# Two attention layers on one core: all casts to fp16 on GpSimd, the remainders' subtractions spread over later steps, and scores issued ahead of the row sums

## The chip, the cores and the metric

The program runs on 1 NeuronCore of a Trainium2 chip. The metric is the device time of one execution in microseconds; before and after are each run several times, and the median counts.

## The reference, cut to what matters

The input is 8 images of 512 channels by 32 x 32 positions (1024 tokens). Two attention layers follow each other. Layer 0 has 8 heads of 64 channels with quantized q, k and v; layer 1 has a single head over all 512 channels.

```python
# layer 0, per image: xf is (512, 1024)
h = group_norm(xf, gn_w, gn_b)
qkv = einsum('oc,bct->bot', qkv_w, h) + qkv_b
q, k, v = (fake_quant(t) for t in split(qkv))     # 8 bits, one scale over all images
w = softmax(einsum('bct,bcs->bts', q * scale, k * scale))
a = einsum('bts,bcs->bct', w, v)
x = xf + proj_w @ a + proj_b
# layer 1, per image
t = group_norm(x).reshape(B, C, H * W).transpose(0, 2, 1)
q, k, v = t @ wq.T + bq, t @ wk.T + bk, t @ wv.T + bv
out = softmax(q @ k.T / sqrt(C)) @ v
x = x + (out @ wp.T + bp)
```

## The kernel before, in words

The program has three parts. The first (up to about 640 us) normalizes all images, computes layer 0's q, k and v, stores them in device memory and gathers the extremes that the quantization needs; it is not touched by the change. The second and third are one interleaved stream: layer 0's attention, written as a Python generator `attention()`, and everything else (first the folding of layer 1's weights, `fold()`, then per image layer 0's output projection, `project`, the normalization `norm1`, and layer 1, `layer1`), written as generators too. Around 790 us the folding is over; until then the variable `alone` is true.

**Attention's units.** A unit is one image b, one pair of heads j, one half hf of the queries (512 of them) and one of 8 blocks s of 128 keys. There are 8 x 4 x 2 x 8 = 512 units. For each one:

- `scores` (L770 and above): two matmuls, one for each head of the pair, give `st`, 128 keys x 2 x 512 queries, in PSUM. ScalarE's exponential (L770) writes it to SBUF as `pt` in fp32. The pool of `st` tiles has two buffers, so the third unit's scores wait for the first one's exponential.
- the split: `pt` is cast to fp16 (L777), and VectorE subtracts the cast from `pt` (L778), again to fp16. The two fp16 parts together, tile `two`, stand for the fp32 value. The cast is on ScalarE for even s; for odd s it is on GpSimd, or on VectorE while `alone`.
- `weighted`: four matmuls per unit multiply both parts by v (`av`), and four sum them over the keys with a matrix of ones (`sm`), the softmax's denominators.
- `finish`, after the 8th block: ScalarE copies `av` and `sm` out of PSUM, and the division follows (L832), put off by some steps.

**Bursts.** The generator yields after every four units. One such step, a burst, issues the scores of two units, the `av` and `sm` matmuls of the four units of the burst before, and the scores of two more units. A burst that falls into the projection or the normalization is `dense` and is ordered in two halves of two units. In layer 1, the function `run` calls a burst where a block of products has reached a listed step.

**Layer 1's blocks.** Each matrix product of layer 1 is a 2 x 2 block scheme with seven products (`seven`), which accumulate in two PSUM banks x and y by turns. Between them ScalarE copies a bank to `kept_u` (L1055, L1092, L1188), and VectorE adds bank y and a kept copy into the result (L1068 for `g`, L1110 for `v`, L1125 for `p`, L1159 for the output). TensorE's next product but one into the same bank waits until that add has read it. In the list of products: the add for bank y of products 0 and 1 comes before product 3; the next before product 6; the last before the next block's product 1.

**Chores.** Work that can wait is put in a list by `later(name, delay, work)`, with the step at which it is due, and `chore()` takes the first entry that is due; `settle(name)` does all that is left under a name. While `alone`, `later` does the work at once. Quantization (L652, L655), division (L832) and some of the sums of layer 1 are chores. The splits of a burst's third and fourth unit are chores under the name "sum", due at once, cast and subtraction together; those of the first and second are issued right with their scores.

TensorE runs its instructions in the order in which the source issues them: `mm` (L106) ties each matmul to the last. On the other engines the framework's scheduler may order the queue otherwise than the source[...].

Of the kernel before, what the change touches and what calls it, by code (L numbers as in the profile page):

```python
# [9 lines left out]
F32 = mybir.dt.float32  # L10
BF = mybir.dt.bfloat16
F16 = mybir.dt.float16
I32 = mybir.dt.int32
AF = mybir.ActivationFunctionType
ALU = mybir.AluOpType
AX = mybir.AxisListType

P = 128
# [3 lines left out]
NT = T // P  # L22
# [31 lines left out]
def attn_pair_kernel(  # L54
# [9 lines left out]
    nc = tc.nc  # L64
# [5 lines left out]
    const = ctx.enter_context(tc.tile_pool(name="const", bufs=1))  # L70
# [26 lines left out]
            sq = slice(r, r + 32)  # L97
            nc.vector.tensor_tensor(gavg[sq, sq], low[sq, :], low_t[sq, :], ALU.is_equal)
    nc.vector.tensor_scalar(gavg, gavg, 1.0 / GS, None, ALU.mult)
    ident = const.tile([P, P], F32, name="ident")  # L100
    make_identity(nc, ident)

    last_mm = [None]

# [78 lines left out]
    with ExitStack() as fast:  # L183
# [84 lines left out]
        with tc.tile_pool(name="p1w", bufs=1) as p1w, tc.tile_pool(name="p1", bufs=3) as p1, tc.tile_pool(  # L268
            name="p1o", bufs=4
# [271 lines left out]
            for t in range(2 * PAIRS):  # L541
                isk, j = divmod(t, PAIRS)
# [96 lines left out]


        qkp = fast.enter_context(tc.tile_pool(name="qkp", bufs=2))
        ptp = fast.enter_context(tc.tile_pool(name="ptp", bufs=3))
        partp = fast.enter_context(tc.tile_pool(name="partp", bufs=6))
        aop = fast.enter_context(tc.tile_pool(name="aop", bufs=5))
        l2p = fast.enter_context(tc.tile_pool(name="l2p", bufs=1))
# [74 lines left out]
        chores = []  # L720
        now = 0

        def later(name, delay, work):
            if alone:
                work()
            else:
                chores.append((name, now + delay, work))

        def chore(passed=1):
            nonlocal now  # L730
            now += passed
            for i, (_, due, work) in enumerate(chores):
                if due <= now:
                    del chores[i]
                    work()
                    break

        def settle(what):

# [6 lines left out]
        def attention():  # L746

            units = [(b, j, hf, s) for b in range(B) for j in range(PAIRS) for hf in range(NH)
                     for s in range(NT)]
            pairs = {}
            pairs[0, 0] = load_pair(0, 0)
            parts, avs, sms, rss = {}, {}, {}, {}

            def scores(u, wait=False):
                b, j, hf, s = units[u]
                if hf == 0 and s == 0:
                    settle("quant")  # L760
                nm = f"{b}_{j}_{hf}"
                qt, kt, _ = pairs[b, j]
                st = pair_ps(f"st_{nm}_{s}")
                for i, r in enumerate(HALF):
                    mm(
                        st[:, i, :], lhsT=kt[r, bass.ts(s, P)],
                        rhs=qt[r, bass.ts(hf, 512)], start=True, stop=True,
                    )
                pt = ptp.tile([P, 2, 512], F32, tag="p", name=f"pt_{nm}_{s}")
                nc.scalar.activation(pt, st, AF.Exp, scale=esc)  # L770
                parts[u] = two = partp.tile([P, 2, 2, 512], F16, tag="two", name=f"two_{nm}_{s}")
                cast = nc.scalar.copy
                if s % 2:
                    cast = nc.vector.tensor_copy if alone else nc.gpsimd.tensor_copy

                def split():
                    cast(two[:, 0], pt)  # L777
                    nc.vector.tensor_tensor(two[:, 1], pt, two[:, 0], ALU.subtract)  # L778

                if wait:  # L780
                    later("sum", 0, split)
                else:
                    split()

            def weighted(us):
                for u in us:
                    b, j, hf, s = units[u]
                    if s == 0:
                        avs[b, j, hf] = av_bank(f"av_{b}_{j}_{hf}")
                    for w in range(2):  # L790
                        for i, r in enumerate(HALF):
                            mm(
                                avs[b, j, hf][r, :], lhsT=pairs[b, j][2][:, s, r],
                                rhs=parts[u][:, w, i, :], start=(s == 0 and w == 0),
                                stop=(s == NT - 1 and w == 1),
                            )
                for u in us:
                    b, j, hf, s = units[u]
                    if s == 0:
                        sms[b, j, hf] = av_bank(f"sm_{b}_{j}_{hf}")  # L800
                    two = parts.pop(u)
                    for n in range(4):
                        mm(
                            sms[b, j, hf][n * QUAD : (n + 1) * QUAD, :], lhsT=ones16,
                            rhs=two[:, n // 2, n % 2, :], start=(s == 0), stop=(s == NT - 1),
                        )

            def finish(b, j, hf):

                nm = f"{b}_{j}"  # L810
                if hf == 0:
                    ao[b, j] = aop.tile([P, NH, 512], F32, tag="ao", name=f"ao_{nm}")
                    rss[b, j] = l1p.tile([P, NH, 512], F32, tag="rs", name=f"rs_{nm}")
                aot, rs = ao[b, j], rss[b, j]
                nc.scalar.copy(aot[:, hf, :], avs.pop((b, j, hf)))
                nc.scalar.copy(rs[:, hf, :], sms.pop((b, j, hf)))
                if hf == 0:
                    return
                del rss[b, j]
                n = b * PAIRS + j  # L820

                apart = small.tile([P, 2, 16], F32, tag="apart", name=f"apart_{nm}")
                for w in range(2):
                    nc.sync.dma_start(
                        apart[:, w, :],
                        rs[2 * w * QUAD : 2 * (w + 1) * QUAD : QUAD].rearrange(
                            "r h (p k) -> r h p k", k=16
                        ),
                    )

                def divide():
                    nc.vector.scalar_tensor_tensor(aot, aot, scl[:, 2:3], rs, ALU.mult, ALU.mult)  # L832

                def spread():
                    r = rcs[:, n * 16 : (n + 1) * 16]
                    nc.vector.tensor_add(r, apart[:, 0, :], apart[:, 1, :])
                    nc.vector.reciprocal(r, r)
                    nc.sync.dma_start(rs_d[n].rearrange("r (p k) -> (r p) k", k=16), r)
                    for i, r in enumerate(HALF):
                        nc.sync.dma_start(  # L840
                            rs[r], rs_d[n][2 * i : 2 * i + 2, :].partition_broadcast(CH)
                        )
                    later("ao", 5, divide)

                later("ao", 4, spread)

            scores(0)
            scores(1)
            yield 9.0, 0
            scores(2)  # L850
            scores(3)
            yield 9.0, 0
            for u in range(0, len(units), 4):
                b, j, hf, s = units[u]
                settle("sum")
                if hf == 0 and s == 0:
                    n = b * PAIRS + j + 1
                    if n < B * PAIRS:
                        pairs[divmod(n, PAIRS)] = load_pair(*divmod(n, PAIRS))

                if u + 4 < len(units):
                    scores(u + 4)
                    scores(u + 5)
                weighted((u, u + 1) if dense else range(u, u + 4))
                late = dense
                for n in range(2):
                    if n == late:
                        if dense:  # L870
                            weighted((u + 2, u + 3))
                        if s == NT - 4:
                            finish(b, j, hf)
                    if n == 0 and u + 4 < len(units):
                        scores(u + 6, wait=True)
                        scores(u + 7, wait=True)
                chore(0)
                last = (j, hf, s) == (PAIRS - 1, NH - 1, NT - 4)
                yield 6.0 + (hf == NH - 1 and s == NT - 4), b + last
# [258 lines left out]
        def o_run(b, hf, vt, vs, ps_, pts, acc, rx, between):  # L1138
# [11 lines left out]
            nm = f"o2_{b}_{hf}"  # L1150
            spare = done >= B
            u = kept(nm, spare)
# [32 lines left out]
            for step in seven(  # L1185
# [20 lines left out]
                elif step == 6:  # L1206
# [6 lines left out]
                        check_sums()  # L1213
                    if (1, 0) not in rx:
                        load_x1(b, hf, 1, 0, rx)
                if step != 6:
                    chore(2)
            finish(1)
            settle("o")

# [11 lines left out]
        def run(*blocks, at=(5,)):  # L1232

            for steps in zip(*blocks):
                if steps[0] in at:
                    yield 1
                if len(blocks) > 1 and steps[0] == 6:
                    for _ in range(3):
                        chore(0)
                elif steps[0] not in (5, 6):  # L1240
                    chore()

        def layer1(b, steps):

# [182 lines left out]
        alone = True  # L1427
# [403 lines left out]
```

## Time and profile before

| | |
|---|---|
| time, median of 3 runs | 2819.06 us (2813.53 to 2820.5) |
| profiled execution | 2813.1 us span |
| TensorE busy | 2621.5 us, 93% |
| VectorE busy | 1924.6 us, 68% |
| ScalarE busy | 1152.1 us, 41% |
| GpSimd busy | 280.9 us, 10% |
| subtractions of the split (L778) | 512, mean 1236 ns, 617.1 us |
| exponentials (L770) | 512, mean 1124 ns, 554.7 us |
| casts on ScalarE, GpSimd, VectorE (L777) | 256, mean 1055 ns; 218, mean 1197 ns; 38, median 686 ns |

PE is TensorE, PEld its loading of weights, DVE is VectorE, ACT is ScalarE, POOL is GpSimd. A busy share is an average over stages with different limits; the ends of matmuls are modelled, and spans on GpSimd are rough. A span on VectorE or GpSimd can contain time in which the instruction was held up after it had begun. The page also names, for idle time, what ended it.

### The profile page before, as it was taken

Reading aid. Unit: us, or ns where it says so; the run is one execution under the profiler, and the core shown is the slowest. Engines: PE = TensorE matmul, PEld = TensorE weight load, DVE = VectorE, ACT = ScalarE, POOL = GpSimd, SP = SyncE. Lnnn points to the kernel's source line nnn. Section 1 sums busy time; section 2 is a strip of 40 time slices with the busy share of each in tenths; the row PEclk is TensorE's granted clock in tenths of the full one; section 3 lists DMA queues with packets and bytes.
Section 4 is the critical chain, followed back from the end, with each engine's and each line's share of the span. In section 5 each row is a group of like instructions: output and inputs, shape, how many; then the busy total and the mean of one; then the engine's idle time right before and its main releaser. Section 6 shows DMA issues by size and latency. Waiting matters only on the chain.

```text
span 2813.1 us, 33256 instructions
## 1 busy us (share of the span) xinstructions
PE 2621.5 (93%) x13110; PEld 1650.1 (59%) x13110; DVE 1924.6 (68%) x2772; ACT 1152.1 (41%) x1474; POOL 280.9 (10%) x248
## 2 busy tenths in 40 slices
PE   7999999997779999999999999999999999999998
PEld 3455555552226665665566566656665665567687
DVE  6766665668987767776776677677767766764534
ACT  0011111117955563645465455535563645463021
POOL 0000000000011111111111111111111111110000
PEclk9999999999999999999999999999999999999999
DMA  5233322333321223123212421241233123201401
GB/s 195 101 120 120 113 112 90 120 118 122 106 87 31 72 85 107 54 72 117 76 39 64 128 72 39 85 131 44 73 92 98 52 72 113 71 10 46 142 8 43
DMA packets 147461, 241.94 MB, mean 86 GB/s; under 512 B 26592, under 2 KB 92128, under 8 KB 145760
## 3 DMA queue, kind: packets, MB, share of 16 engines
q1 hardware_dynamic: 116448, 181.50, 19.5%
q10 hardware_dynamic: 30848, 58.23, 6.3%
q8 instruction: 104, 1.70, 0.3%
q14 instruction: 61, 0.50, 0.1%
HBM read 152.86 MB, written 86.28 MB: 85 GB/s over the span
## 4 chain that ended last, share of the span: by engine, by line
PE 50%; DVE 22%; issue 11%; ACT 10%; DMA 5%; POOL 1%; ACTq 0%; SPq 0%; DVEq 0%; POOLq 0%
PE s L106 10%; PE qkps L106 10%; DVE two L778 9%; PE o L106 7%; ACT pt L770 5%; PE pj L106 5%; PE vps L106 5%; PE v2ps L106 4%; PE g L106 4%; ACT two L777 3%; PE av L106 3%; DMA rs<-rs_d 2%; PE st L106 2%; PE sm L106 1%; DVE ao L832 1%
## 5 line engine op out<-in xcount | busy, mean ns | idle before, releaser
L778 DVE TENSOR_TENSOR two<-pt,two 128x1024 f16<-128x1024 f32 x512 | 617.1, 1236 | 254.8 <-ACT two L777 240.4
L770 ACT ACTIVATE pt<-st,esc 128x1024 f32<-128x1024 f32 x512 | 554.7, 1124 | 214.9 <-PE st L106 168.8
L777 POOL CAST two<-pt 128x1024 f16<-128x1024 f32 x218 | 260.9, 1197 | 1537.5 <-ACT pt L770 1531.7
L777 ACT CAST two<-pt 128x1024 f16<-128x1024 f32 x256 | 270.0, 1055 | 1.1
L106 PE MATMUL av<-two,v 128*64 128x512 f16 x2048 | 255.9, 388 | 0.3
L398 ACT ACTIVATE u<-qkps,qkb 128x512 f32<-128x512 f32 x84 | 57.7, 687 | 476.5 <-PE qkps L106 472.1
L106 PE MATMUL s<-g,h 128*128 128x256 f32 x1024 | 238.2, 382 | 13.7 <-DVE p L1125 10.1
L106 PE MATMUL pj<-ao,wp 128*128 128x512 f32 x512 | 223.0, 594 | 0.0
L106 PEld LDWEIGHTS s<-g,h 128*128 128x128 f32 x1024 | 191.7, 190 | 51.1 <-DVE p L1125 16.6
L106 PE MATMUL st<-q,k 64*128 64x512 bf16 x1024 | 166.1, 386 | 56.6 <-ACT pt L770 44.1
L106 PE MATMUL s<-g,sums 128*128 128x256 f32 x768 | 183.7, 386 | 14.3 <-ACT kept_u L1092 14.3
L106 PEld LDWEIGHTS <-v 128*64 128x64 f16 x2048 | 104.5, 110 | 134.4 <-issue 62.5
L106 PE MATMUL o<-p,v 128*128 128x256 f32 x768 | 174.1, 382 | 0.0
L106 PEld LDWEIGHTS s<-g,sums 128*128 128x128 f32 x768 | 142.0, 190 | 50.0 <-ACT kept_u L1092 22.7
L106 PE MATMUL qkps<-x,wqkv 128*128 128x512 f32 x352 | 165.4, 613 | 2.2 <-DVE x L155 2.2
L106 PEld LDWEIGHTS pj<-ao,wp 128*128 128x128 f32 x512 | 96.6, 190 | 119.0 <-issue 115.2
L106 PEld LDWEIGHTS o<-p,v 128*128 128x128 f32 x768 | 144.2, 190 | 27.2 <-issue 8.5
L106 PE MATMUL g<-h,wa 128*128 128x256 f32 x512 | 127.8, 394 | 30.7 <-DVE kept_u L1159 14.4
L106 PE MATMUL qkps<-sums,wa 128*128 128x512 f32 x336 | 153.3, 592 | 0.0
L106 PE MATMUL sm<-two,ones 128*32 128x512 f16 x2048 | 141.2, 387 | 0.0
L106 PEld LDWEIGHTS <-k 64*128 64x128 bf16 x1024 | 35.2, 94 | 174.3 <-issue 173.7
L106 PE MATMUL v2ps<-wm,h 128*128 128x256 f32 x512 | 121.9, 385 | 10.9 <-DVE v L1110 6.6
(218 smaller groups left out, 3530.6 us busy)
## 6 DMA issues: line engine op xcount, KB each, us to landing
rs<-rs_d SPq DMA_DIRECT2D x80, 256.0 KB
x<-in_x_dram SPq DMA_DIRECT2D x32, 512.0 KB
raw<-q_d SPq DMA_DIRECT2D x32, 512.0 KB
raw<-k_d SPq DMA_DIRECT2D x32, 512.0 KB
raw<-v_d SPq DMA_DIRECT2D x32, 512.0 KB
x_d<-h SPq DMA_DIRECT2D x64, 256.0 KB
x<-x_d ACTq DMA_DIRECT2D x64, 256.0 KB
out_dram<-x SPq DMA_DIRECT2D x64, 256.0 KB
```

Of the source, the lines that this page charges most:

```text
L106: ins = nc.tensor.matmul(*args, **kw).ins
L398: nc.scalar.activation(dst, x, AF.Identity, bias=bias)
L770: nc.scalar.activation(pt, st, AF.Exp, scale=esc)
L777: cast(two[:, 0], pt)
L778: nc.vector.tensor_tensor(two[:, 1], pt, two[:, 0], ALU.subtract)
L832: nc.vector.scalar_tensor_tensor(aot, aot, scl[:, 2:3], rs, ALU.mult, ALU.mult)
```

## The change

Five edits, made together.

- All casts of the split go to GpSimd; only while `alone` the odd ones are on ScalarE. None is on VectorE.
- `scores` no longer splits. A new function `split(u, delay)` issues the cast at once and puts the subtraction into the chores under "sum" with a delay: 0 for the burst's first two units, 1 for the other two.
- `chore` may now do several entries in a call: as many "sum" entries as steps have passed (at least one), and one entry of any other name unless it is called with `quiet`. Steps of a block that had no chore call now have a quiet one, so that a subtraction can stand there.
- `weighted` is divided into `over_keys` (the `av` matmuls) and `totals` (the `sm` matmuls). In a burst that isn't dense, the scores of the third and fourth unit are issued between the two, ahead of the row sums.
- The pool of `pt` tiles has four buffers instead of three, and an identity tile of the first part that nothing in this path read is gone.

It is meant to free ScalarE of the casts, to keep the subtractions from standing in front of layer 1's adds on VectorE, and to let the last two exponentials of a burst begin earlier.

```diff
-        ptp = fast.enter_context(tc.tile_pool(name="ptp", bufs=3))
+        ptp = fast.enter_context(tc.tile_pool(name="ptp", bufs=4))
...
-        def chore(passed=1):
+        def chore(passed=1, quiet=False):
             nonlocal now
             now += passed
-            for i, (_, due, work) in enumerate(chores):
-                if due <= now:
-                    del chores[i]
-                    work()
-                    break
+            for n in range(max(passed, 1) + (not quiet)):
+                for i, (name, due, work) in enumerate(chores):
+                    if due <= now and (name == "sum") == (n < max(passed, 1)):
+                        del chores[i]
+                        work()
+                        break
...
-                parts[u] = two = partp.tile([P, 2, 2, 512], F16, tag="two", name=f"two_{nm}_{s}")
-                cast = nc.scalar.copy
-                if s % 2:
-                    cast = nc.vector.tensor_copy if alone else nc.gpsimd.tensor_copy
-
-                def split():
-                    cast(two[:, 0], pt)
-                    nc.vector.tensor_tensor(two[:, 1], pt, two[:, 0], ALU.subtract)
-
-                if wait:
-                    later("sum", 0, split)
-                else:
-                    split()
+                pts[u] = pt
+
+            def split(u, delay):
+                b, j, hf, s = units[u]
+                pt = pts.pop(u)
+                two = partp.tile([P, 2, 2, 512], F16, tag="two", name=f"two_{b}_{j}_{hf}_{s}")
+                parts[u] = two
+                cast = nc.scalar.copy if alone and s % 2 else nc.gpsimd.tensor_copy
+                cast(two[:, 0], pt)
+                later("sum", delay, lambda: nc.vector.tensor_tensor(
+                    two[:, 1], pt, two[:, 0], ALU.subtract
+                ))
...
-                weighted((u, u + 1) if dense else range(u, u + 4))
-                late = dense
-                for n in range(2):
-                    if n == late:
-                        if dense:
-                            weighted((u + 2, u + 3))
-                        if s == NT - 4:
-                            finish(b, j, hf)
-                    if n == 0 and u + 4 < len(units):
-                        scores(u + 6, wait=True)
-                        scores(u + 7, wait=True)
+                two_scores(u + 4)
+                if dense:
+                    over_keys((u, u + 1))
+                    totals((u, u + 1))
+                    two_splits(u + 4, 0)
+                    two_scores(u + 6)
+                    over_keys((u + 2, u + 3))
+                    totals((u + 2, u + 3))
+                else:
+                    over_keys(range(u, u + 4))
+                    two_scores(u + 6)
+                    totals(range(u, u + 4))
+                    two_splits(u + 4, 0)
+                if s == NT - 4:
+                    finish(b, j, hf)
+                two_splits(u + 6, 1)
                 chore(0)
...
-                if step != 6:
-                    chore(2)
+                chore(2, quiet=step == 6)
...
-                elif steps[0] not in (5, 6):
-                    chore()
+                else:
+                    chore(quiet=steps[0] in (5, 6))
```

## The prediction

> **What bounds the kernel now.** I read the page's busy line first, then busy time by stretches of time, then TensorE's waits, then groups of instructions by form, then the timeline of single bursts. The columns are: engine shares on the page; in the stretches the length, then PE, PEld, DVE, ACT and POOL busy with counts, clock, DMA share and GB/s; in the waits total us, times, longest.
>
> ```profile
> PE 2621.5 (93%) x13110; PEld 1650.1 (59%) x13110; DVE 1924.6 (68%) x2772; ACT 1152.1 (41%) x1474; POOL 280.9 (10%) x248
> ...
> 640.00:790.00 150.00, 112.28 (x805) 37.32 (x802) 143.37 (x170) 128.92 (x139) 0.00 (x0) 0.94 0.31 103
> ...
> 1381.00:1642.00 261.00, 244.23 (x1382) 160.11 (x1379) 184.44 (x230) 133.76 (x170) 39.08 (x33) 0.99 0.26 79
> ```
>
> TensorE bounds the whole (93%), but there are two regimes. From 640 to 790 us attention runs almost alone: VectorE is busy 143.37 of 150 us, TensorE only 112.28, so VectorE is the limit there. From 800 us on, an image repeats every 261 us with TensorE at 244 and VectorE at 184. TensorE's own waits from 800 us to the end name VectorE or ScalarE as the releaser:
>
> ```profile
> PE sm_l L106 <- DVE acc L1293: 19.0, 7, 2.7
> PE g L106 <- DVE kept_u L1159: 14.4, 13, 2.0
> PE s L106 <- ACT kept_u L1092: 14.3, 21, 0.7
> PE s L106 <- DVE p L1125: 10.1, 13, 1.3
> ```
>
> So layer 1's products stop now and then for an add on VectorE (L1125, L1110, L1159, L1068: they empty a PSUM bank that the next product but one overwrites). Little of that is lost now, but the adds are just in time. One burst of the repeating image, with its columns start, length, engine, line, operation, tiles, shape, count, idle time before:
>
> ```profile
> 1448.42 0.60 PE L106 MATMUL st<-q,k 64*128 64x512 bf16 x4
> ...
> 1449.01 2.13 ACT L770 ACTIVATE pt<-st,esc 128x1024 f32<-128x1024 f32 x2
> ...
> 1451.01 1.05 ACT L777 CAST two<-pt 128x1024 f16<-128x1024 f32 x1
> 1451.19 1.38 POOL L777 CAST two<-pt 128x1024 f16<-128x1024 f32 x1 [9.90 <-ACT pt L770]
> ...
> 1452.10 2.68 DVE L778 TENSOR_TENSOR two<-pt,two 128x1024 f16<-128x1024 f32 x2 [0.43 <-ACT two L777]
> ...
> 1454.70 0.68 DVE L1125 TENSOR_TENSOR p<-s,kept_u 128x512 f32<-128x512 f32 x1
> ```
>
> Two exponentials, one cast on ScalarE beside one on GpSimd, two subtractions, then the add that TensorE needs, 6.96 us after the burst's first matmul; the third product needs it at 7.7. The other two casts and subtractions come behind that add.
>
> And how GpSimd and VectorE meet (q, k quantization and a cast; then division, cast, and an add out of PSUM):
>
> ```profile
> 1439.65 0.75 DVE L655 TENSOR_SCALAR q<-raw,bhi 128x1024 bf16<-128x1024 f32 x1
> 1439.87 1.43 POOL L777 CAST two<-pt 128x1024 f16<-128x1024 f32 x1 [2.36 <-ACT pt L770]
> 1440.31 1.53 DVE L655 TENSOR_SCALAR k<-raw,bhi 128x1024 bf16<-128x1024 f32 x1
> ...
> 1414.09 1.28 DVE L832 SCALAR_TENSOR_TENSOR ao<-ao,scl,rs 128x1024 f32<-128x1024 f32 x1
> ...
> 1414.31 1.96 POOL L777 CAST two<-pt 128x1024 f16<-128x1024 f32 x1 [2.36 <-ACT pt L770]
> 1415.29 0.68 DVE L1110 TENSOR_TENSOR v<-v2ps,kept_u 128x512 f32<-128x512 f32 x1
> ```
>
> The cast alone takes 1.04 us. Started during q (which ends at 1440.40) it ends at 1441.30, 0.90 after q; k, caught behind it, takes 1.53 instead of 0.75 and ends 0.54 after the cast. The cast behind the division ends 0.90 after it too (1415.37, 1416.27), while the add out of PSUM runs its normal 0.68 within that cast. So SBUF work of the two engines goes one at a time. In the burst above the first subtraction ends about 1.07 after the cast that held it (1452.57; the pair ends at 1454.78, the second takes 1.14).
>
> [...]
>
> **The change part by part.** The counts: of 512 casts, 256 are on ScalarE (mean 1055 ns), 218 on GpSimd and 38 on VectorE (0.687 us).
>
> *Stretch alone.* The 38 VectorE casts go (38 x 0.687 = 26.1 us), the 38 even ones move from ScalarE to GpSimd and the odd ones to ScalarE, whose load stays. GpSimd's 38 casts hold the lock 0.90 us each, 34.2 us; subtractions behind a cast are about 0.08 shorter (38 x 0.08 = 3.0). VectorE and lock together: 143.4 - 26.1 + 34.2 - 3.0 = 148.5 us, at the same 95.6% use 155 us: +5 us. Ends: 0 (perfect packing) to +15 (each cast 1.04 and a gap). The fourth pt buffer takes away ScalarE's waits for subtractions here (8.3 us), but ScalarE isn't the limit.
>
> *Order on TensorE.* Scores of units 3 and 4 move ahead of the row sums, from 3.36 us after the burst's start (1451.78) to 2.38, where the row sums began (1450.80). The second exponential ends at 1451.14, 2.72 after the start, and frees the score bank for the fourth unit, which is wanted at about 2.62: TensorE waits some 0.17 us. 16 bursts an image: 2.7 us. Behind it stand the row sums and layer 1's next product.
>
> *Casts and subtractions.* All four casts of a burst now stand in GpSimd's queue, all four subtractions behind them in VectorE's, and alternate through the lock. First exponential over at +1.7, cast to 2.82, then four times 1.07 and three times 0.90: the fourth subtraction ends at 9.8 us. Each quantization between them adds about 0.6, a division 1.1. Before, with two casts on ScalarE, the fourth ended at 9.4 in a plain burst, with quantizations and divisions in VectorE's idle time (it waits 35.7 us an image for ScalarE's casts). The built order decides the rest: subtractions are put off in the source, but in the program's VectorE queue most bursts have all four in front of layer 1's add; before, in several bursts the add stood behind the second or third. Behind the subtraction wait the add, behind that ScalarE's copy or exponential, and TensorE. Per image, add's end after against when TensorE wants it, less the wait of before:
> - Three bursts early in a block, where the third product on wants the add: v block, division between (10.4 against 7.9): 2.5. s block, v quantization between (11.1 against 7.9): 3.2. o block, three quantizations (12.4 against 10.0): 2.4.
> - Four late in a block, where the next block's second product wants it (at about 10.2 after the burst's start): 1.45, 1.3, 1.75 and 1.85.
> - Six in the middle, where before is just in time as well: 0.6, 0.45, 0.35, 0.2, 0, 0; 1.6 in all.
> - One amid the normalization[...]: about 2.2.
> - Two inside the projection: 0, its 14 us of matmuls hide them.
> Sum 18.3, with the banks' 2.7 it is 21 us on 261. (512 - 76) / 64 = 6.8 images, less some 20 units that run within the first projection and normalization: 6.5 x 21 = 137 us.
>
> *The rest.* ScalarE loses 34 us of casts an image; it was 51% busy and its copies mostly waited for TensorE, so I count 0. The removed identity tile: 0, it is in the start, not on a path. Extra calls of the chore queue only order the work.
>
> Sum: 2819 + 137 + 5 = 2961, say 2960.
>
> **Rivals.** (1) The casts hide: if the lock cost nothing, four subtractions would end at 2.85 + 4 x 1.14 = 7.4 instead of 9.4, and TensorE's waits on those adds (14.4 + 10.1 + 8.2 + 3.7 = 36 us) would go, the stretch alone would lose up to 20 us, against 18 for the banks: about 2780. For it: VectorE waits long for ScalarE's casts now. Against: every meeting in the trace shows the lock. (2) Layer 1's products have more slack than I see, the add comes out just in time as now, and only the banks (18), the stretch alone (5) and some adds count: 2830 to 2880. For it: the subtractions are meant to come behind the adds. Against: the built order. (3) VectorE with the lock becomes the bound: delays carry from burst to burst, 1.5 times the loss, about 3035. Against: an image has 184 + 32 x 0.9 = 213 of 261 us.
>
> **How the numbers follow.** Forecast (2880 to 3020) 0.65; rival 2 0.17; rival 3 0.05; no measurable change 0.03; rival 1 0.10. Slower 0.87. The low end takes in most of rival 2, the high end the lock at its full 1.04 and 1.16 us a piece (fourth subtraction at 10.6, 0.8 later in 13 bursts of 6.5 images: +68).
>
> **What would show it.** Right: TensorE's waits on L1125, L1110, L1159 and L1068 (their new lines) grow to over 100 us in all; casts and subtractions alternate with spans near 1.9 us; an image takes about 282 us; a small new wait of st for pt in most bursts; the stretch alone is no shorter. Wrong: adds finish within 10 us of a burst's start, casts and subtractions overlap freely, or an image stays at 261 us.

## The result, and the profile after

The changed kernel takes 3074.91 us (median of 4 runs, 3074.46 to 3078.45) against 2819.78 us before (2813.53 to 2820.93): ratio 1.0912, 95% interval 1.0894 to 1.0931. The direction is as predicted. The time is 115 us above the forecast of 2960 and 55 us above the range.

First the page of the changed kernel: busy time by engine, and the two groups of the split.

```profile
PE 2729.2 (89%) x13110; PEld 1712.9 (56%) x13110; DVE 2124.0 (69%) x2734; ACT 945.8 (31%) x1256; POOL 702.5 (23%) x502
...
L781 POOL CAST two<-pt 128x1024 f16<-128x1024 f32 x474 | 683.3, 1464 | 1377.2 <-ACT pt L771 1356.8
L782 DVE TENSOR_TENSOR two<-pt,two 128x1024 f16<-128x1024 f32 x512 | 798.4, 1599 | 224.3 <-POOL two L781 224.0
```

A subtraction takes 1599 ns instead of 1236, a cast on GpSimd 1464 instead of 1197. What the prediction calls the lock is in these spans: of the 512 subtractions 284 meet a cast, and they average 1.91 us against 1.21 for the others; the 401 casts that meet an operation of VectorE average 1.54 against 1.04 for the 73 that meet none. The prediction's "SBUF work of the two engines goes one at a time" is too wide, though: in the three meetings of the normalization's statistics (L939) with a cast, they overlap by 0.26 to 0.39 us and neither is longer (0.69 and 1.04 us), while the normalization's own TENSOR_SCALAR (L153) takes 1.04 us in the mean of its 21 meetings and 0.54 otherwise. The second thing to see is TensorE's busy time. It grew by 108 us (2621.5 before) though the 13110 matmuls are the same ones. Most of that is a slower clock, and some is that matmuls overlap less; both are worked out below. The stretches of time show the clock (length, then PE, PEld, DVE, ACT and POOL busy with counts, granted clock, DMA share, GB/s):

```profile
640.00:790.00 150.00, 114.59 (x795) 38.21 (x794) 142.98 (x130) 123.63 (x135) 60.00 (x37) 0.95 0.31 99
...
1381.00:1642.00 261.00, 221.97 (x1151) 143.17 (x1150) 183.52 (x205) 83.56 (x112) 74.64 (x54) 0.93 0.23 67
```

The clock in the second line was 0.99 before. An image now repeats every 300 us; one whole image, from its first burst to the next image's, first in the kernel before and then in the changed one:

```profile
1512.03:1775.13 263.10, 246.38 (x1398) 161.04 (x1398) 186.03 (x233) 135.35 (x172) 39.68 (x33) 0.99 0.26 79
...
1623.86:1924.19 300.33, 259.10 (x1398) 168.56 (x1398) 214.12 (x232) 105.24 (x140) 91.93 (x65) 0.96 0.23 69
```

The same 1398 matmuls take 37 us longer: 24.5 are idle time of TensorE (41.2 against 16.7) and 12.7 are longer busy time. The waits behind the idle time, from 640 us on (total us, times, longest):

```profile
PE v2ps L104 <- DVE v L1124: 39.6, 14, 3.8
PE g L104 <- DVE kept_u L1173: 36.7, 13, 3.6
PE s L104 <- DVE p L1139: 32.4, 14, 3.4
...
PE st L104 <- ACT pt L771: 26.1, 58, 0.8
PE av L104 <- DVE two L782: 21.8, 25, 1.7
```

The last two lines lie in good part in the stretch alone. From 785 us on, scores wait 12.6 us for their bank (32 times; before 8.5 us, 12 times), and `av` waits 3.6 us.

The same burst as the one shown of before (there TensorE didn't wait), with columns as there:

```profile
1546.32 0.61 PE L104 MATMUL st<-q,k 64*128 64x512 bf16 x4
...
1548.93 0.39 PE L104 MATMUL st<-q,k 64*128 64x512 bf16 x2 [0.15 <-ACT pt L771]
1548.94 2.04 POOL L781 CAST two<-pt 128x1024 f16<-128x1024 f32 x2 [10.40 <-ACT pt L771]
...
1549.93 0.39 PE L104 MATMUL st<-q,k 64*128 64x512 bf16 x2 [0.61 <-ACT pt L771]
...
1550.02 4.02 DVE L782 TENSOR_TENSOR two<-pt,two 128x1024 f16<-128x1024 f32 x2 [1.18 <-POOL two L781]
...
1551.44 3.50 POOL L781 CAST two<-pt 128x1024 f16<-128x1024 f32 x2 [0.45 <-ACT pt L771]
...
1553.96 1.52 DVE L653 TENSOR_SCALAR v<-raw,bhi 128x1024 f16<-128x1024 f32 x1
...
1555.40 2.34 DVE L782 TENSOR_TENSOR two<-pt,two 128x1024 f16<-128x1024 f32 x2
...
1557.67 0.68 DVE L1139 TENSOR_TENSOR p<-s,kept_u 128x512 f32<-128x512 f32 x1
...
1558.40 3.78 PE L104 MATMUL s<-g,sums 128*128 128x256 f32 x8 [3.45 <-DVE p L1139]
```

Two casts take 2.04 us undisturbed, the next two 3.50; two subtractions take 4.02; the quantization of v takes 1.52 instead of 0.75; the add begins 11.35 us after the burst's start, and TensorE has waited 3.45 us. Then comes what I had not reckoned with: its next eight matmuls take 3.78 us where eight take 1.89 to 1.99 elsewhere. In the records of the kernels before and after, the 136 changes of the granted clock lie whole multiples of 3.41 us apart. The same moments cut at these steps of the clock:

```profile
1553.61:1557.02 3.41, 1.34 (x7) 0.84 (x5) 3.41 (x4) 0.59 (x1) 1.32 (x1) 1.00 0.15 26
1557.02:1560.44 3.42, 2.04 (x5) 1.68 (x6) 3.39 (x6) 0.63 (x1) 0.00 (x0) 0.50 0.40 132
1560.44:1563.85 3.41, 3.41 (x10) 2.69 (x9) 0.08 (x1) 0.00 (x0) 0.00 (x0) 0.50 0.17 43
1563.85:1567.26 3.41, 3.41 (x27) 1.54 (x26) 0.69 (x1) 2.37 (x4) 0.71 (x1) 1.00 0.43 118
```

A step in which TensorE was busy 1.34 us of 3.41 is followed by two at half clock (0.50), and in the second of these it is busy all the time: waiting is over, and it still runs slowly.

From the first projection matmul (at 784.6 us before, 785.0 after) to the end, TensorE's gaps add up to 128.6 us before and 281.4 after, and half of the time spent at half clock to 13.7 and 105.8. So 152.8 us are new stalls and 92.1 the clock: 244.9 of the 258.9 us by which this part grew. (The clock's sum is a little too large: time at half clock in which TensorE was idle anyway stands in both sums. It is 7.4 of the 105.8 us.) Where the other 14 us lie is shown with the order of the scores below.

### The profile page after: what moved, and what is told of

Its sections match the earlier page's. It is cut to its first block, busy times and chain, and to the rows that moved or that the text cites. A ratio compares the mean times of both kernels' runs of the same rounds, so it can differ in the third digit from the quotient of the medians.

```text
span 3072.4 us, 33616 instructions
## 1 busy us (share of the span) xinstructions
PE 2729.2 (89%) x13110; PEld 1712.9 (56%) x13110; DVE 2124.0 (69%) x2734; ACT 945.8 (31%) x1256; POOL 702.5 (23%) x502
## 4 chain that ended last, share of the span: by engine, by line
PE 36%; DVE 24%; issue 24%; POOL 6%; DMA 6%; ACT 5%; SPq 0%; ACTq 0%; POOLq 0%; DVEq 0%
DVE two L782 12%; PE qkps L104 9%; POOL two L781 5%; PE pj L104 5%; PE s L104 5%; PE o L104 5%; PE vps L104 4%; ACT pt L771 4%; PE g L104 4%; PE v2ps L104 3%; DMA rs<-rs_d 2%; DMA raw<-q_d 1%; DMA raw<-k_d 1%; DVE q L653 1%; DVE raw L650 1%
## 5 line engine op out<-in xcount | busy, mean ns | idle before, releaser
L781 POOL CAST two<-pt 128x1024 f16<-128x1024 f32 x474 | 683.3, 1464 | 1377.2 <-ACT pt L771 1356.8
L782 DVE TENSOR_TENSOR two<-pt,two 128x1024 f16<-128x1024 f32 x512 | 798.4, 1599 | 224.3 <-POOL two L781 224.0
L771 ACT ACTIVATE pt<-st,esc 128x1024 f32<-128x1024 f32 x512 | 545.7, 1122 | 249.7 <-PE st L104 212.3
L104 PE MATMUL av<-two,v 128*64 128x512 f16 x2048 | 260.1, 387 | 22.5 <-DVE two L782 21.8
L104 PE MATMUL s<-g,h 128*128 128x256 f32 x1024 | 250.0, 395 | 26.2 <-DVE v L1124 15.8
L104 PE MATMUL pj<-ao,wp 128*128 128x512 f32 x512 | 237.3, 621 | 19.3 <-DVE h L936 19.3
L104 PE MATMUL s<-g,sums 128*128 128x256 f32 x768 | 196.8, 404 | 38.5 <-DVE p L1139 23.5
L104 PE MATMUL st<-q,k 64*128 64x512 bf16 x1024 | 179.9, 386 | 37.4 <-ACT pt L771 27.9
L104 PE MATMUL g<-h,wa 128*128 128x256 f32 x512 | 143.2, 429 | 51.9 <-DVE kept_u L1173 36.7
L104 PE MATMUL v2ps<-wm,h 128*128 128x256 f32 x512 | 135.8, 417 | 34.4 <-DVE v L1124 17.8
L104 PEld LDWEIGHTS g<-h,wa 128*128 128x128 f32 x512 | 105.0, 212 | 84.4 <-DVE kept_u L1173 42.0
```

The source lines that it names most:

```text
L104: ins = nc.tensor.matmul(*args, **kw).ins
L782: later("sum", delay, lambda: nc.vector.tensor_tensor(two[:, 1], pt, two[:, 0], ALU.subtract))
```

## The experiments

Theory A: casts on GpSimd and subtractions on VectorE wait for each other by turns, TensorE's stalls for the adds grow, and stalls of two microseconds and more cost half clock besides. Rival B: the new order of scores and row sums, or the new times of the chores, makes the loss. Rival C: four casts in a row on any one engine. "Idle" and "clock" below are the two sums just named, for each run. They stand at 128.6 and 13.7 us before, 281.4 and 105.8 after.

**The casts undone** (the rest of the change kept).

```diff
-                cast = nc.scalar.copy if alone and s % 2 else nc.gpsimd.tensor_copy
+                cast = nc.scalar.copy
+                if s % 2:
+                    cast = nc.vector.tensor_copy if alone else nc.gpsimd.tensor_copy
```

> The changed kernel with one part undone: the casts are placed as before (even blocks on ScalarE, odd ones on GpSimd, odd ones on VectorE while attention runs alone); order of scores and row sums, delays, chores and the fourth pt buffer stay changed. Theory A ([...]TensorE's stalls for the adds grow, and stalls of about 2 us and more cost half clock besides): back near the kernel before, 2790 to 2840 us, mean clock 0.985 or more, subtractions near 1.25 us. Rival B (the new order of scores and row sums and the new times of the chores make the loss): stays at 2980 us or more.

Measured: 2850.16 us, ratio to before 1.0134 (1.0110 to 1.0158); idle 140.4, clock 22.2. It is 10 us above A's figure and far below B's. 225 of the 255 us go with the casts.

**The casts alone** (the same edit the other way round, in the kernel before).

> The kernel before with one part of the change: all casts on GpSimd (ScalarE for odd blocks while attention runs alone), nothing else changed. Theory A: most of the loss is here, 2980 to 3060 us, mean clock 0.975 or less, subtractions near 1.6 us. Rival B: at most 2850 us.

Measured: 3015.04 us, 1.0720 (1.0695 to 1.0745); idle 257.0, clock 75.1; subtractions 1556 ns. As A has it: the casts by themselves make 199 us, the rest by itself 34, and some 20 come from both together. B is out as the main cause.

**The order of the scores undone.**

```diff
                     over_keys(range(u, u + 4))
-                    two_scores(u + 6)
                     totals(range(u, u + 4))
+                    two_scores(u + 6)
```

> The changed kernel with the scores of the third and fourth unit put back behind the row sums; casts, delays and chores stay changed. Theory A (casts and lock, then the clock): the waits of scores for a bank (26 us) go and nothing else, 3040 to 3075 us. Rival B (order of scores and row sums): below 2950 us.

Measured: 3017.91 us, 1.0712 (1.0694 to 1.0730); idle 262.4, clock 71.7. That is 57 us less than the changed kernel, between the figures of the two theories. By the two sums, 19 are idle time and 34 the clock. The waits for the bank don't turn the clock down themselves: in the changed kernel, of the 51 times that the clock fell from 785 us on, none followed a step with such a wait in it. What differs is the number of TensorE's stalls of over 2 us in that part: 72 in the changed kernel, 53 here, 10 before. The score matmuls show one cost more. Their lines on the pages of before, of the changed kernel and of this run (busy time, mean ns of one, idle time before them):

```profile
L106 PE MATMUL st<-q,k 64*128 64x512 bf16 x1024 | 166.1, 386 | 56.6 <-ACT pt L770 44.1
...
L104 PE MATMUL st<-q,k 64*128 64x512 bf16 x1024 | 179.9, 386 | 37.4 <-ACT pt L771 27.9
...
L104 PE MATMUL st<-q,k 64*128 64x512 bf16 x1024 | 165.2, 386 | 25.9 <-ACT pt L771 16.2
```

One matmul takes the same 386 ns, but with the scores ahead they overlap less and fill 14 us more. In the burst above, the third and fourth unit's take 0.39 us for each pair, because each pair waits for its own bank; the four of the burst's first two units take 0.61 together.

**Chores alone**: both edits, the casts as before and the scores behind the row sums.

> The changed kernel with the casts placed as before and the scores of the third and fourth unit back behind the row sums: what is left of the change is the delayed subtractions, the new chore rules, the split function and the fourth pt buffer. If the order of scores and row sums made the 34 us by which the run with the casts as before was slower: 2810 to 2830 us. If the chores made it: 2840 to 2855 us.

Measured: 2824.71 us, 1.0022 (1.0013 to 1.0031). So the order of the scores makes 25 us with the casts as before, and split, delays, chores and the fourth buffer together 7.

**All casts on ScalarE.**

```diff
-                cast = nc.scalar.copy if alone and s % 2 else nc.gpsimd.tensor_copy
+                cast = nc.scalar.copy
+                if alone and s % 2 == 0:
+                    cast = nc.gpsimd.tensor_copy
```

> The changed kernel with all casts on ScalarE once attention no longer runs alone; GpSimd does none there. A cast alone takes about 1.05 us on either engine. Theory A (lock): subtractions back at 1.2 us, the fourth ends about 2 us earlier in the burst, 2790 to 2880 us. Rival C (what hurts is that one engine casts all four in a row, lock or not): 2950 us or more, here with ScalarE's copies behind the casts.

Measured: 2906.03 us, 1.0326 (1.0299 to 1.0353); idle 181.0, clock 35.8; subtractions 1241 ns. Between the two figures. The subtractions no longer wait for casts in their spans, but ScalarE's copies out of PSUM stand behind casts: TensorE waits 30.9 us for the copy of an s block (15.0 in the changed kernel). Inconclusive about C.

**All casts on VectorE.**

```diff
-                cast = nc.scalar.copy if alone and s % 2 else nc.gpsimd.tensor_copy
+                cast = nc.vector.tensor_copy
+                if alone:
+                    cast = nc.scalar.copy if s % 2 else nc.gpsimd.tensor_copy
```

> The changed kernel with all casts on VectorE itself once attention no longer runs alone (0.69 us each there). Four casts and four subtractions still go one after another, but no engine hands a lock to another: 4 x (0.69 + 1.14) = 7.3 us for them instead of 4 x (0.90 + 1.07) = 7.9, and nothing else of VectorE's is held up by a cast. Theory A (the lock): the fourth subtraction ends about 0.7 us earlier, quantizations and divisions are not stretched; idle falls by 40 to 90 us, clock term by 40 to 60, 2900 to 2990 us. Rival C (a chain of eight in a row is what counts, whatever the engine): 3040 us or more, as VectorE is 41 us per image busier.

Measured: 2824.43 us, 1.0018 (1.0006 to 1.0031); idle 117.8, clock 13.7. Below both figures: putting the casts on the busiest of the engines in question takes away 250 of 255 us. Rival C, which foretold 3040 us or more, is out as the main cause. The burst of above in this kernel's timeline:

```profile
1715.88 0.60 PE L104 MATMUL st<-q,k 64*128 64x512 bf16 x4
...
1720.14 0.75 DVE L653 TENSOR_SCALAR v<-raw,bhi 128x1024 f16<-128x1024 f32 x1
...
1722.54 0.69 DVE L783 CAST two<-pt 128x1024 f16<-128x1024 f32 x1
1723.15 0.68 DVE L1141 TENSOR_TENSOR p<-s,kept_u 128x512 f32<-128x512 f32 x1
1723.75 1.21 DVE L784 TENSOR_TENSOR two<-pt,two 128x1024 f16<-128x1024 f32 x1
...
1723.88 1.99 PE L104 MATMUL s<-g,sums 128*128 128x256 f32 x8 [0.17 <-DVE p L1141]
```

The quantization takes 0.75 again and the add begins at 7.27 us, TensorE waits 0.17. But the add also stands in front of two subtractions here, which it doesn't in the changed kernel. Lock and order are mixed in this run, so neither this result nor the next settles the share of each. The cast by itself is shorter here too, 0.69 us against 1.04 alone on GpSimd.

**Subtractions behind the adds** (casts on GpSimd; `ins` is the subtraction, `last_add` the last layer 1 add issued before it).

```diff
+                    if last_add[0] is not None:
+                        tc.add_manual_dep(ins, last_add[0].name, IN_ORDER, reason="order")
```

> The changed kernel, and each subtraction is kept behind the last layer 1 add issued before it in the source, so that the fourth (in some bursts the third too) stands behind the add in VectorE's queue. All casts stay on GpSimd. Theory A with the order as its second half (the lock makes the chain long, and the add has to wait for the whole of it): the add leaves about 2 us earlier, most stalls fall under 1.5 us, 2840 to 2930 us, mean clock above 0.975. If the lock's chain alone sets the pace, the next burst's av products wait instead: 3000 us or more.

Measured: 3015.11 us, 1.0710 (1.0686 to 1.0734); idle 258.6, clock 64.8. The order alone gives back 60 us of 255, two thirds of it clock, and TensorE's waits of `av` for subtractions rise from 21.8 to 32.2 us. My figure for it was far too low; the time lies in the band of the second outcome, but these waits grew by only 10 us.

**Order held, engine changed.** Each subtraction issued with its cast and each add tied behind the last subtraction, so that all four stand ahead of the add in both kernels; casts on GpSimd in one and on VectorE in the other.

```diff
+                if last_sub[0] is not None:
+                    tc.add_manual_dep(last_tt[0], last_sub[0].name, IN_ORDER, reason="order")
```

> The changed kernel, with each subtraction issued right with its cast and each layer 1 add kept behind the last subtraction issued before it in the source, so that all four subtractions of a burst stand ahead of its add in VectorE's queue. All casts on GpSimd. The order is nearly that of the changed kernel as built: 3060 to 3120 us, mean clock 0.965 or less. It serves to be set against the next run.

> The same forced order, but all casts on VectorE itself once attention no longer runs alone. Lock (the alternation of GpSimd's casts with VectorE's subtractions is what costs, the order only carries it to TensorE): 2830 to 2890 us. Order (the run with the casts on VectorE was fast because the framework put the add ahead of some subtractions there): 2950 us or more.

Measured: 3106.63 us, 1.0995 (1.0955 to 1.1036), idle 302.1, clock 119.5, with GpSimd; 2893.69 us, 1.0263 (1.0241 to 1.0285), idle 160.3, clock 46.1, with VectorE (4 us above my band). An image of the first:

```profile
1644.61:1950.53 305.92, 262.51 (x1397) 170.84 (x1396) 214.40 (x232) 105.23 (x140) 90.77 (x65) 0.95 0.22 68
```

and of the second:

```profile
1543.66:1822.08 278.42, 254.37 (x1398) 166.41 (x1398) 216.07 (x296) 105.34 (x140) 1.01 (x1) 0.97 0.24 75
```

VectorE's busy time is the same, 214 and 216 us, for 232 operations in the first and for 296 in the second, where 64 casts are among them. By an estimate, these make 44 us at 0.69 each, so the other 232 fill about 172; in the first run they last some 42 us longer, as operations that meet a cast do above. With all four subtractions in front of the add, the engine of the casts makes 213 us; with casts on VectorE, the forced order makes 69 (2893.69 against 2824.43). So the engine leads, and the order has a part. The 213 us contain that GpSimd's cast is slower (1.04 us alone against 0.69) as well as that it alternates with VectorE; no run takes the two apart here. The run with all casts on ScalarE speaks for the alternation: at 1.05 us a cast, as slow as GpSimd's, but without the alternation, it was 169 us faster than the changed kernel, although TensorE waited longer for ScalarE's copies. Its order of subtractions and adds wasn't held, though. In the two runs with the order held, that is the order of subtractions against adds alone; casts, quantizations and divisions fell where they fell.

**Stalls of known size, no GpSimd in it.** In the kernel before, VectorE's add of an s block is issued three or six times with the same operands.

```diff
-                tt(dst, ps, u, ALU.add)
+                for _ in range(6):
+                    tt(dst, ps, u, ALU.add)
```

> The kernel before (casts, order and all), with VectorE's add of an s block issued three times with the same operands: the same result, and each add leaves 1.2 us later. It puts a stall of known size on TensorE without touching GpSimd. There are 96 such adds. Theory K (a stretch of 3.41 us in which TensorE is idle for over about 1.9 us is followed by one at half clock): idle grows by at most 115 us and stays in pieces below 1.9 us, so the clock term grows by less than 20 us; 2870 to 2930 us. Rival G (the clock falls because of GpSimd's work): no clock change here or with six.

> The same with the add issued six times: each leaves 3.05 us later, stalls of 2.5 us and more. Theory K: idle grows by 200 to 290 us and most stalls are followed by half clock, so some 80 to 130 us are lost to the clock besides, mean clock 0.96 or less; 3100 to 3220 us, and the clock term grows by far more than in proportion to the doses (5 against 2 added adds). Rival G: clock stays at 0.99, 3010 to 3110 us.

Measured: 2930.30 us, 1.0401 (1.0384 to 1.0419), and 3167.12 us, 1.1243 (1.1224 to 1.1262). One image with three adds:

```profile
1551.57:1831.18 279.61, 251.43 (x1397) 163.41 (x1397) 201.17 (x257) 134.78 (x172) 39.96 (x33) 0.98 0.24 74
```

and with six:

```profile
1633.52:1944.17 310.65, 263.31 (x1398) 171.12 (x1398) 223.21 (x293) 135.63 (x172) 39.17 (x33) 0.92 0.21 67
```

GpSimd's busy time is that of before; the clock falls to 0.92. Idle rises by 77.6 and 228.1 us, the clock term by 25.6 and 150.1. Of the 150.1, 38 us fell into time in which TensorE was idle anyway; with these left out (0.5 of the 25.6), three times the idle time brings 4.5 times the loss of clock. With three adds the clock term is above my figure (less than 20), and the time at the upper end of the band. The two sums explain 103 of the 115 us by which this part grew with three adds. Rival G is out: the clock follows the length of the stalls, not GpSimd.

**Better than both.** The kernel before with its odd casts on VectorE throughout.

```diff
-                    cast = nc.vector.tensor_copy if alone else nc.gpsimd.tensor_copy
+                    cast = nc.vector.tensor_copy
```

> The kernel before with the casts of odd blocks on VectorE throughout (0.69 us each) instead of GpSimd; ScalarE keeps the even ones. VectorE gets 22 us busier per image, and the lock is gone. If the lock costs the kernel before anything worth having: 2780 to 2810 us. If VectorE's added work only makes the adds later: 2830 to 2900 us.

Measured: 2780.54 us, 0.9864 (0.9836 to 0.9892); idle 95.1, clock 10.2. Its page:

```profile
PE 2620.6 (94%) x13110; PEld 1648.7 (59%) x13110; DVE 1999.3 (72%) x2990; ACT 1152.6 (41%) x1474; POOL 20.4 (1%) x30
```

VectorE is 75 us busier, and the whole 37 us faster (2818.01 beside it).

The same with the fourth `pt` buffer (`bufs=4`) and without the unused identity tile:

> The kernel before with the casts of odd blocks on VectorE and the fourth pt buffer. If ScalarE's exponentials still wait for a pt buffer where it matters: 2760 to 2775 us; if not, as without the fourth buffer, 2777 to 2785 us.

Measured: 2780.98 us, 0.9857 (0.9832 to 0.9881): the fourth buffer adds nothing.

The kernel before with the fourth buffer and the tie of the run with subtractions behind the adds:

> The kernel before with the fourth pt buffer, and each subtraction kept behind the last layer 1 add issued before it in the source (as in the run with subtractions behind the adds); casts and order as before. If the adds' place in VectorE's queue is worth what TensorE waits for them before (about 36 us in all): 2780 to 2810 us. If the late subtractions then hold up the next burst's av products: 2820 to 2860 us.

Measured: 2828.15 us, 1.0046 (1.0032 to 1.0060). The second of the two outcomes: TensorE now waits 51.2 us for late subtractions at `av`, 41.9 of them from 785 us on. Keeping subtractions back by hand doesn't pay when the next burst wants them.

## Why the prediction was wrong, by its own steps

- *Stretch alone, +5 us*: right. From the first score matmul to the first projection matmul it is 144.9 us before and 149.4 after.
- *Order on TensorE, 18 us*: right in size, in part by luck. Undoing it takes 19 us of idle time away in the changed kernel, but from 785 us on the waits for the bank fall by only 11 of them (12.6 to 1.5); the rest are stalls elsewhere. The step had a short wait in every burst and did not have the 14 us by which the score matmuls overlap less. In time the order is 25 us with the old casts and 57 with the new, where more of the other stalls last over 2 us.
- *Casts and subtractions, the fourth ending at 9.8 us, some 0.6 later per quantization*: right. The earliest fourth subtraction in 109 bursts ends 9.88 us after its burst's start, the median 10.64. The scores ahead did bring the fourth exponential from 6.64 to 5.25 us (medians); the alternation used that up, since before the fourth subtraction ended at 10.69 too. The difference is what had to wait for it: two or three subtractions stood ahead of the add in several bursts of before, mostly four after.
- *Stalls, 21 us an image*: right. Averaged over five images, TensorE's idle time per image is 17.3 us before and 40.6 after: 23.3 more. The two bursts with the clearest working: division between, forecast 2.5, measured 2.6; s block with v's quantization, forecast 3.2, measured 3.45 at the add (4.3 with the waits of that burst's scores).
- *282 us an image; sum 2960*: here it fails. The step multiplied the stalls by 6.5 images and took that for the whole loss, with the matmuls at their old length. Each image is 13 us longer by the clock as well, 92 us over the part. The term was put at nothing, without being named. The forecast of 142 us (137 + 5) stands against 157 (152.8 + 4.5) of stalls measured; with the clock's 92 the forecast would have been 3052. The two sums leave 14 us over, and these lie in the score matmuls: from 785 us on they fill 136.7 us before and 150.6 in the changed kernel. In all seven kernels with the scores ahead they fill 12 to 14 us more than before in the time at full clock alone; in all others they stay within 1.5 us of before. The run with three adds, in the order of before, has 12 us left over for a like reason: TensorE stops 212 times instead of 155, and a layer 1 matmul right after a stop adds 0.48 us to the busy time where one in a row adds 0.22. With six adds the sums overshoot by 28, for the 38 us counted twice.
- *The range*: its upper end took in a dearer lock, but every case in it priced a stall at its own length, so all of them were too low together.
- *Rivals*: the third, at 3035, came nearest in time and has the wrong cause: VectorE is busy 214 of 300 us. The first and second are out by the time itself.
- *Signs*: the waits on the adds came to 157 us in their six largest groups (over 100 foretold), casts and subtractions alternate with spans near 1.9 us, the stretch alone is no shorter, and the small wait of scores for the bank grows, but to 32 times in 109 bursts (0.39 us each), not in most. The image's length was off: 300 us, not 282.

The clue was in the lines that I showed. A clock of 0.94 stood in the stretch alone, where TensorE was busy 112 of 150 us, and 0.99 beside it where stalls were short. I left the clock out of a sum in which I had stalls of 2.4 to 3.2 us.

## What to carry to other kernels

A stall of TensorE had two prices here: its length (152.8 us in all), and the clock of what followed (92.1 us, 60% more). Ask of each new stall whether it makes TensorE idle for more than about 2 us within one of the clock's steps of 3.41 us: all 385 such steps at full clock in the runs here were followed by one at half clock. And before moving an elementwise operation to an idle engine, look in the trace at which operations of other engines it has to take turns with: here 128x1024 casts were best on VectorE at 0.69 us, though it was the busier engine, and worst on GpSimd, where they alternated with its subtractions (1.04 us alone, 1.46 in the mean of the changed kernel).

## What the runs showed of the hardware that I had not expected

Over the records of all sixteen kernels profiled here, cut into the clock's steps of 3.41 us, from the first step at half clock after 640 us to the last matmul:

| TensorE idle in a step | steps | next at half clock |
|---|---|---|
| at full clock, under 1.4 us | 9230 | 2 |
| 1.4 to 1.7 | 251 | 19 |
| 1.7 to 2.0 | 156 | 45 |
| over 2.0 | 385 | 385 |
| at half clock, under 0.3 us | 432 | 4 |
| 0.3 to 0.6 | 46 | 7 |
| over 0.6 | 114 | 114 |

So the records show two edges: a step at full clock with over 2.0 us of idle time was followed by one at half clock each time (385 of 385), one with less than 1.4 us almost never (2 of 9230); and at half clock the next step stayed there after every step with over 0.6 us of idle time (114 of 114), after one with less than 0.3 us 4 times in 432. A stall of 2 to 3 us is enough where over 2.0 us of it fall within one step, and the same stall costs nothing in one image and 1.7 us or 3.4 (half of one or two steps) in another. The stall of 3.45 us shown above was followed by two steps at half clock in three images of the changed kernel, where 2.04, 2.07 and 2.46 us of it lay on one side of a border between two steps, and by none in three others, where the larger part was 1.75, 1.83 and 1.88 us.
